# One kernel, its front's norm halves and weight sums issued in other rounds, and one more PSUM bank for the last chunk of rows

## The chip, the cores and the metric

The kernel runs on one core of one Trainium2 chip. The metric is the time of one execution on the device in microseconds (us); the time before is the median of three runs. A profile is one more execution, recorded by the hardware profiler; its times count from the start of its span.

The engines have short names in the profile: PE is TensorE (matmuls; PEld is its weight load, which overlaps them), DVE is VectorE, ACT is ScalarE, POOL is GpSimd, SP is SyncE, whose queue issues nearly all transfers here.

## The reference

A residual stack of four layers over `x` of shape 2 x 2048 x 256, in float32. Each layer norms its input and adds its result to `x`:

```python
x = x + scan_layer(layernorm(x), gamma, w_qkva)       # rmsnorm, q*scan(sigmoid(a), kv)
x = x + ffn(layernorm(x), W1, b1, W2, b2)             # 256 -> 1024 -> gelu -> 256
x = x + linear_attention(layernorm(x), W_q, W_k, W_v, W_o)   # 16 heads of 64, a running state
x = x + ffn(layernorm(x), W1, b1, W2, b2)
```

In `ffn` the weights are ternary: each is rounded to -1, 0 or 1 after division by the mean of the absolute values.

## The kernel before

The 4096 rows are 32 chunks of 128 rows. Four chunks make a block of 512 rows, and there are eight blocks, which alternate between the two batches (`blocks`, line 110). All of `x` stays on the chip in `x_sb`, each layer adding to it in place.

There are three parts. `front` (lines 557 to 738) does the scan layer and the first ffn. `attention` (lines 748 to 1196) does the third layer in 32 steps and begins the last ffn. A loop at the end (lines 1346 to 1367) does the rest of the last ffn. In all three PE, DVE, ACT and POOL execute their instructions in the order in which the code issues them (`by_hand`, line 1314), save for a few statistics that the program builder draws forward; only SP's transfers are ordered by a scheduler. So where a call stands in the code is where its instructions stand in each engine's queue, and an instruction that waits holds up all behind it on its engine.

The second half of `front` is a loop over eight rounds `i` (line 670). Round `i` does the ffn of block `i`:

- `ffn_in` (line 502): eight steps `f`, each with four matmuls of 128x512 into one bank (line 509), then the gelu on ACT (line 515). After each second step the 128x1024 result `h` is split: ACT casts it to `hh` (line 488), DVE subtracts to get the rest `hl` (line 494). Two buffers `h` take turns, so the gelu of steps 4 and 5 waits until the first `hl` is done.
- `ffn_out` (line 520): eight steps of eight matmuls (line 531), each of a step's four chunks with `hh` and with `hl`, into two banks of two chunks. DVE adds the banks to `x_sb` (line 540). In the last block of the last ffn the order is different: chunks 0 to 2 run through all eight `f` first, then chunk 3 alone, and each bank is added and stored as soon as it is complete. There chunk 2 and chunk 3 are the halves of one bank.
- `ffn_bias` (line 545): POOL adds `b2` to the rows of the next block, one 128x1024 instruction.

The input of `ffn_in` is made rounds ahead by four calls. `fs_` takes the statistics (four pairs of small DVE instructions, then four small ones on POOL, the last of which, `nb`, line 180, ACT waits for). `fr_`, in `fq_`, lets ACT write the normed rows `xn` (line 194). `fq_` goes on to turn them: DVE transposes 32x32 squares (line 259), SP writes them to DRAM in one transfer and reads them back in four. `fe_` splits what came back into halves: ACT casts to `xh` (line 202), DVE subtracts to `xl` (line 203). The halves of blocks 3 and 5 lie in the room of the weight `wq`, which is loaded from DRAM when round 5 has read them (line 704).

In rounds 0 to 3 the scan layer of later blocks is woven in; rounds 4 to 7 are the ffn alone.

Attention multiplies by a seven-product scheme (`Seven`, line 773). It needs sums of its weights: `weights_kv` (line 462) makes four POOL instructions of 128x512 for each of `wk`, `wv`, `wq`. They are issued in `ffn_out` of rounds 4, 5 and 6 (line 712, through the list at line 1330). It also needs sums `S` of the normed input (`pair_sums`, line 760: four POOL instructions of 128x128). The first of these stand at the start of attention; they wait for the last round's matmuls, since `S` takes over room that `hl` had. The first three products that PE does there are `hkN_Y` and `hkN_X`, which need no sum, and then `hkN_Z`, which needs the first of `S` and of `wk_t`.

Attention's own first rows (the chunk pair 0) are made in `front` by three calls: `then[0]` is `attention_stats` in round 6 after four steps of `ffn_in`, `then[1]` is `attention_rows` in `ffn_out` of round 6 (ACT writes two `xn`, DVE transposes them into `first_squares`, SP writes and reads back), and `then[2]` is `attention_turned` in round 7 (ACT copies to `xnT_first`). The statistics of the second pair of chunks are taken at the start of attention (line 994); their four small POOL instructions follow those of `S`.

Of the kernel before, what the change touches and what calls it, by code (L numbers as in the profile page):

```python
# [20 lines left out]
ALU = mybir.AluOpType  # L21
AX = mybir.AxisListType

P = 128
B, T, D = 2, 2048, 256
ND = D // P
FF = 4 * D
NF = FF // P
# [16 lines left out]
def kernel(  # L45
# [15 lines left out]
    nc = tc.nc  # L61
# [25 lines left out]
    wq = None  # L87
    wk = const.tile([P, ND, H * DK], FP, tag="wk", name="wk")
    w2 = const.tile([P, NF, D], FP, tag="wv", name="w2_in")
    wv = None  # L90
# [352 lines left out]
    def ffn_weights_away():  # L443

        for nm, w in (("w1r", w1r), ("w2r", w2r)):
            kept[nm] = dram.tile(w.shape, FP, tag=f"d{nm}", name=f"d{nm}")
            nc.sync.dma_start(out=kept[nm], in_=w.bitcast(FP))
# [14 lines left out]
    def weights_kv(w, t):  # L462
        l, r = slice(0, HK), slice(HK, H * DK)
        B11, B12, B21, B22 = w[:, 0, l], w[:, 0, r], w[:, 1, l], w[:, 1, r]
        T1, T2, T3, T4 = t[:, 0, :], t[:, 1, :], B12, t[:, 2, :]
        nc.gpsimd.tensor_tensor(T1, B12, B11, ALU.subtract)
        nc.gpsimd.tensor_tensor(T2, B22, T1, ALU.subtract)
        nc.gpsimd.tensor_tensor(T3, B22, B12, ALU.subtract)
        nc.gpsimd.tensor_tensor(T4, B21, T2, ALU.subtract)
# [50 lines left out]
    def ffn_out(g0, hid, store=False, tag="ps"):  # L520

        banks = [bank([P, 2, D], f"o{g0}_{i}", tag) for i in range(2)]
        if store and g0 == blocks[-1]:
            order = [(f, range(BC - 1)) for f in range(NF)] + [(f, range(BC - 1, BC)) for f in range(NF)]
        else:
            order = [(f, range(BC)) for f in range(NF)]
        for f, cs in order:
            for c in cs:
                to = banks[c // 2][:, c % 2, :]
                for k, h in enumerate((hid.hi, hid.lo)):  # L530
                    nc.tensor.matmul(  # L531
                        to, lhsT=h[f // 2][:, f % 2, c * P : (c + 1) * P], rhs=w2r[:, f, :],
                        start=(f == 0 and k == 0 and c % 2 == 0), stop=(f == NF - 1 and k == 1),
                        skip_group_check=True,
                    )
                m = 1 if len(cs) < BC and c > 1 else 2
                if f == NF - 1 and (c % 2 == 1 or m == 1):
                    g = g0 + c + 1 - m
                    xs = x_sb[:, g : g + m, :]
                    nc.vector.tensor_tensor(xs, xs, banks[c // 2][:, c % 2 + 1 - m : c % 2 + 1, :], ALU.add)  # L540
                    if store:
                        nc.sync.dma_start(out=rows(of, g, m), in_=xs)
            yield

    def ffn_bias(g0):

        xs = x_sb[:, g0 : g0 + BC, :]
        nc.gpsimd.tensor_tensor(xs, xs, b2_sb.unsqueeze(1).to_broadcast([P, BC, D]), ALU.add)

    def run(steps, n=None):  # L550
        for _ in steps if n is None else zip(range(n), steps):
            pass
# [4 lines left out]
    def front(scan_pool, ffn_pool, tern_pool, then, later):  # L557
# [21 lines left out]
        def fs_(i, between=None):  # L579
            fst[i] = norm_stats(ffn_pool, chunks(blocks[i]), bias=True, between=between)  # L580
# [4 lines left out]
        def fq_(i, to=ffn_pool, tag="raw"):  # L585
            fr_(i)
            src = fn[i].rearrange("t c (d b i) -> t b (c d) i", d=ND, b=NQ)
            nm = f"xn{blocks[i]}"
            fn[i] = squares_in(to, nm, squares_out(ffn_pool, nm, [src], 1), 1 if to is ffn_pool else None, tag)

        def fe_(i):
            if i > 5 and i % 2:
                room = [scan_pool.tile([P, ND, BT], FR, tag="kq", name=f"{t}{blocks[i]}") for t in ("xh", "xl")]
            elif i % 2:
                room = const.tile([P, 2, ND, BT], FR, tag="wq", name=f"xhl{blocks[i]}")
                room = [room[:, k] for k in range(2)]
            else:
                room = rows_room(ffn_pool, blocks[i], bufs=1)
            fn[i] = halves_end(fn[i], room)
# [70 lines left out]
        for i in range(NB):  # L670
            u, g0 = i + 5, blocks[i]
            more, scans = i + 1 < NB, u < len(units)
            hid, staged = hidden(ffn_pool, g0)
            steps = ffn_in(g0, fn.pop(i), hid, staged)
            if i == 0:
                ffn_bias(g0)
            if scans:
                ys[u] = []
                products = scan_steps(scan_pool, units[u][0], xnT[u], last[units[u][0] // CPB], ys[u])
                for j in range(4):  # L680
                    run(products, 1)
                    run(steps, 1)
                    if i == 0 and j == 0:
                        a_(4)
                        fq_(1)
                run(products)
                if i == 3:
                    fq_(5, scan_pool, "xn")
            else:
                run(steps, 4)  # L690
                if i == 4:
                    fs_(7)
                if i == NB - 2:
                    then[0]()
            if u + 1 < len(units):
                s_(u + 1)
            if i == 0:
                fs_(2)
            run(steps)
            if u + 1 < len(units):  # L700
                r_(u + 1)
            if i == 5:
                wq = const.tile([P, ND, H * DK], FP, tag="wq", name="wq")
                nc.sync.dma_start(out=wq, in_=w_q.rearrange("(c p) e -> p c e", p=P))
            if not more:
                wo = const.tile([P, NPR, D], FP, tag="wo", name="wo")
                nc.sync.dma_start(out=wo, in_=w_o.rearrange("(c p) e -> p c e", p=P))
                then[2]()

            steps = ffn_out(g0, hid, tag="out")  # L710
            if i > 3 and i - 4 < len(later):
                later[i - 4]()
            if i == 2:
                ffn_weights_away()
            if scans:
                fe_(i + 1)
                run(steps, 2)
                a_(u)
                run(steps, 3)
                if u + 1 < len(units):  # L720
                    t_(u + 1)
            if i < 3:
                fq_(i + 2)
                fs_(i + 3)
                if i == 2:
                    fs_(6)
            elif i == 3:
                fq_(6)
                fe_(5)
            elif i + 2 < NB:  # L730
                fe_(i + 2)
                if i + 3 < NB:
                    fq_(i + 3)
            if i == NB - 2:
                then[1]()
            run(steps)
            if more:
                ffn_bias(blocks[i + 1])

# [6 lines left out]
    def attention(keep, pool, state, last):  # L748
# [11 lines left out]
        def pair_sums(n):  # L760

            x = pairs[n]
            S = pool.tile([P, 4, P], FP, tag="S", bufs=1, name=f"S{n}")
            l, r = slice(0, P), slice(P, 2 * P)
            x11, x12, x21, x22 = x[:, 0, l], x[:, 1, l], x[:, 0, r], x[:, 1, r]
            for o, a, b_, op in (
                (S[:, 0, :], x21, x22, ALU.add), (S[:, 1, :], S[:, 0, :], x11, ALU.subtract),
                (S[:, 2, :], x11, x21, ALU.subtract), (S[:, 3, :], x12, S[:, 1, :], ALU.subtract),
            ):
                nc.gpsimd.tensor_tensor(o, a, b_, op)  # L770
            pairs[n] = x, S
# [219 lines left out]

        NS = len(steps)
        pair_sums(0)
        stats = norm_stats(norm_pool, pair(1), bias=True)
        k, q, v = Seven(0, "kN", "oT"), Seven(0, "qT", "uT"), Seven(0, "vN", "oT")
        k.go(2, 1, 0, 5)
# [203 lines left out]
    def pair(n):  # L1200
        return [b * CPB + n for b in range(B)]
# [115 lines left out]
    with (  # L1317
        tc.tile_pool(name="scan", bufs=2) as scan_pool,
        tc.tile_pool(name="ffn1", bufs=2) as ffn_pool,
        tc.tile_pool(name="tern", bufs=2) as tern_pool,  # L1320
        tc.manual_schedule(engines=by_hand),
    ):

        warm = bank([P, P], "warm")
        for _ in range(12):
            nc.tensor.matmul(warm, lhsT=ones, rhs=ones, start=True, stop=True)
        nc.scalar.activation(table, ones[:, :1], AF.Sigmoid)
        front(
            scan_pool, ffn_pool, tern_pool, (attention_stats, attention_rows, attention_turned),
            [lambda: weights_kv(wk, wk_t), lambda: weights_kv(wv, wv_t), lambda: weights_kv(wq, wq_t)],  # L1330
        )
    front_ctx.close()

# [71 lines left out]
```

## Time and profile before

| what | us |
|---|---|
| runs | 1059.29, 1057.63, 1059.35 |
| median of the runs | 1059.29 |
| the profiled execution, its own time | 1060.83 |
| its span | 1059.0 |
| round 3, matmuls of `ffn_out` begin | 157.71 |
| rounds 4, 5, 6, 7 begin | 166.06, 182.89, 198.71, 213.64 |
| attention begins | 228.60 |
| last matmul of attention before the last loop, about | 945 |
| last block's `ffn_out` begins | 1046.72 |
| last matmul begins | 1055.54 |

The profile's windows give, for a stretch of time, its length and each engine's busy time in it (in brackets the number of instructions), then the granted TensorE clock, the DMA share and the rate. The timeline gives an instruction's start, its length (of a run of the same ones together, with their number), and in square brackets how long its engine had been idle before it and which instruction ended that. The chain is the work that ended last, each piece followed back to what released it.

### The profile page before, as it was taken

How to read it: one execution, taken by the hardware profiler on the slowest of the kernel's cores; microseconds unless marked ns; L12 is line 12 of the kernel's file. 1: busy time of each engine (PE TensorE's matmuls, PEld its weight loads, DVE VectorE, ACT ScalarE, POOL GpSimd, SP SyncE). 2: the span in 40 equal slices, each digit the busy share in tenths (PEclk: the TensorE clock that was granted, in tenths of full speed). 3: DMA queues.
4: the chain of work that ended last, by engine and by line, in shares of the span. 5: the costliest groups of instructions: out<-in, count | busy, mean ns of one | idle time of the engine just before them, and what ended most of it. 6: DMA issues, size and time to landing. Idle time of an engine off the chain costs nothing.

```text
span 1059.0 us, 43544 instructions
## 1 busy us (share of the span) xinstructions
PE 1044.0 (99%) x19920; PEld 805.4 (76%) x19920; DVE 730.8 (69%) x1047; ACT 613.4 (58%) x813; POOL 201.7 (19%) x314
## 2 busy tenths in 40 slices
PE   9999999999999999999999999999999999999998
PEld 7567778886777777777777777777777777889887
DVE  7987788856676765767666667666576666668873
ACT  4567778755645555455554555545545454658974
POOL 3433242831101001011010110100101020035540
PEclk9999999999999999999999999999999999999999
DMA  9231112203442423423324243243341334223321
GB/s 312 81 119 41 40 41 81 80 20 122 141 135 71 138 95 115 140 77 129 131 75 142 93 132 113 82 133 103 122 136 69 123 122 132 73 82 120 119 81 41
DMA packets 80825, 111.23 MB, mean 105 GB/s; under 512 B 8320, under 2 KB 66560, under 8 KB 80384
## 3 DMA queue, kind: packets, MB, share of 16 engines
q1 hardware_dynamic: 79024, 106.07, 30.2%
q8 instruction: 156, 2.56, 1.0%
q10 hardware_dynamic: 1584, 2.36, 0.9%
q14 instruction: 29, 0.24, 0.1%
q0 software_dynamic: 32, 0.00, 0.0%
HBM read 57.81 MB, written 50.59 MB: 102 GB/s over the span
## 4 chain that ended last, share of the span: by engine, by line
PE 90%; DVE 3%; ACT 2%; issue 2%; DMA 2%; POOL 1%; SPq 0%; ACTq 0%; DVEq 0%
PE hy L952 11%; PE o L531 9%; PE h L509 8%; PE hkN_X L818 6%; PE hqT_X L813 6%; PE hp L872 6%; PE hvN_X L818 6%; PE pq L368 4%; PE pq L388 3%; PE hS L929 3%; PE huT L889 3%; PE hoT L889 3%; PE huT L903 3%; PE hM L929 3%; PE hoT L903 3%; PE hqT_Z L813 3%
## 5 line engine op out<-in xcount | busy, mean ns | idle before, releaser
L878 DVE TENSOR_TENSOR p<-hp,mask 128x512 f32<-128x512 f32 x128 | 82.3, 683 | 83.4 <-PE hp L872 83.4
L952 PE MATMUL hy<-wo,oT 128*128 128x256 f32 x512 | 124.2, 386 | 0.0
L770 POOL TENSOR_TENSOR S<-xnT 128x128 f32<-128x128 f32 x30 | 13.8, 460 | 516.1 <-ACT xnT L312 516.1
L952 PEld LDWEIGHTS hy<-wo,oT 128*128 128x128 f32 x512 | 93.5, 190 | 20.6 <-issue 8.5
L494 DVE TENSOR_TENSOR hl<-h,hh 128x1024 fp32r<-128x1024 f32 x60 | 84.6, 1420 | 29.5 <-ACT hh L488 29.3
L515 ACT ACTIVATE h<-h,b_sb 128x512 f32<-128x512 f32 x120 | 77.9, 683 | 38.6 <-PE h L509 36.1
L914 ACT COPY uT<-huT 128x512 f32<-128x512 f32 x32 | 18.7, 586 | 124.9 <-PE huT L903 124.9
L194 ACT ACTIVATE xn<-x_sb,nb,rs 128x256 f32<-128x256 f32 x124 | 65.7, 594 | 21.9 <-POOL nb L180 20.1
L941 DVE TENSOR_TENSOR S<-S,hS 128x512 f32<-128x512 f32 x60 | 41.2, 687 | 43.2 <-PE hS L929 40.2
L259 DVE STREAM_TRANSPOSE squN<-uT 128x1024 f32<-128x1024 f32 x31 | 63.6, 2053 | 5.4 <-ACT uT L916 4.9
L971 ACT COPY uN<-rawuN 128x1024 f32<-128x1024 f32 x31 | 64.5, 2082 | 4.5 <-DMA rawuN<-dsquN 4.1
L259 DVE STREAM_TRANSPOSE sqkT<-kN 128x1024 f32<-128x1024 f32 x32 | 65.9, 2059 | 1.3 <-ACT kN L849 1.2
L971 ACT COPY kT<-rawkT 128x1024 f32<-128x1024 f32 x32 | 66.7, 2084 | 0.0
L488 ACT CAST hh<-h 128x1024 fp32r<-128x1024 f32 x60 | 63.1, 1051 | 1.9
L531 PE MATMUL o<-w2r,hl 128*128 128x256 f32 x256 | 61.3, 282 | 1.5 <-DVE hl L494 1.3
L531 PE MATMUL o<-w2r,hh 128*128 128x256 f32 x256 | 61.3, 281 | 0.0
L531 PE MATMUL o<-w2r_back,hh 128*128 128x256 f32 x248 | 60.4, 284 | 0.9 <-DVE x_sb L540 0.9
L531 PE MATMUL o<-w2r_back,hl 128*128 128x256 f32 x248 | 60.0, 281 | 0.0
L849 ACT COPY vN<-hvN_X 128x512 f32<-128x512 f32 x16 | 9.4, 587 | 78.8 <-PE hvN_X L818 78.8
L162 DVE BATCH_NORM_STATS2 st<-x_sb 128x6 f32<-128x256 f32 x128 | 51.2, 401 | 2.4 <-DMA x_sb<-in_x_dram 2.3
L823 DVE TENSOR_TENSOR kN<-kN,hkN_Y 128x512 f32<-128x512 f32 x16 | 11.0, 687 | 57.2 <-ACT kN L832 57.2
L531 PEld LDWEIGHTS o<-w2r,hl 128*128 128x128 f32 x256 | 48.2, 188 | 2.9 <-DVE hl L494 2.4
(227 smaller groups left out, 2554.3 us busy)
## 6 DMA issues: line engine op xcount, KB each, us to landing
dsqkT<-sqkT SPq DMA_DIRECT2D x32, 512.0 KB, 3.3
rawkT<-dsqkT SPq DMA_DIRECT2D x128, 128.0 KB, 3.0
dsquN<-squN SPq DMA_DIRECT2D x31, 512.0 KB, 3.3
rawuN<-dsquN SPq DMA_DIRECT2D x124, 128.0 KB, 3.1
dsqxn<-sqxn SPq DMA_DIRECT2D x14, 512.0 KB, 2.7
rawxn<-dsqxn SPq DMA_DIRECT2D x56, 128.0 KB, 2.9
out_dram<-x_sb SPq DMA_DIRECT2D x15, 256.0 KB, 2.9
x_sb<-in_x_dram SPq DMA_DIRECT2D x7, 512.0 KB, 8.9
```

Of the source, the lines that this page charges most:

```text
L194: nc.scalar.activation(xn[:, c, :], x_sb[:, g, :], AF.Identity, bias=nb[:, c : c + 1], scale=rs[:, c : c + 1],)
L259: nc.vector.transpose(to, src)
L494: nc.vector.tensor_tensor(self.lo[a], h, self.hi[a], ALU.subtract)
L509: nc.tensor.matmul(ph, lhsT=w1r[:, d, f * P : (f + 1) * P], rhs=r[:, d, :], start=(d == 0 and k == 0), stop=(d == ND - 1 and k == 1),)
L515: nc.scalar.activation(h[:, f % 2, :], ph, AF.Gelu, bias=b1_sb[:, f : f + 1])
L531: nc.tensor.matmul(to, lhsT=h[f // 2][:, f % 2, c * P : (c + 1) * P], rhs=w2r[:, f, :], start=(f == 0 and k == 0 and c % 2 == 0), stop=(f ...
L813: nc.tensor.matmul(to[:, j, :], lhsT=self.B[i][:, j * P : (j + 1) * P], rhs=self.A[i], start=(new and j == 0), stop=True, skip_group_check ...
L818: nc.tensor.matmul(to, lhsT=self.A[i], rhs=self.B[i], start=new, stop=True, skip_group_check=True)
L872: nc.tensor.matmul(banks[h][halves[c], p, :], lhsT=d[s][left][halves[h], p, halves[c]], rhs=d[s]["qT"][halves[h], p, halves[c]], start=Tru ...
L878: nc.vector.tensor_tensor(d[s][nm][:, h], banks[h], mask8, ALU.mult)
L952: nc.tensor.matmul(py, lhsT=d[s]["oT"][:, p, :], rhs=wo[:, p, :], start=(p == 0), stop=(p == NPR - 1),)
L971: act(t, d[s]["r" + nm].rearrange("p t q -> p q t"))
```

## The change

It has five parts, in the order of the rounds.

1. `fe_(5)` goes from `ffn_out` of round 3 to `ffn_out` of round 4, where `fe_(6)` follows it as before.
2. For block 7, `fs_` goes from the middle of `ffn_in` in round 4 to the start of `ffn_in` in round 5, `fq_` from `ffn_out` of round 4 to that of round 5, and `fe_` from `ffn_out` of round 5 to that of round 6. On SP the load of `wq` now stands before block 7's transfers.
3. `attention_stats` goes from `ffn_in` of round 6 to its `ffn_out`, behind `fe_(7)`; `attention_rows` goes from `ffn_out` of round 6 to `ffn_in` of round 7, behind its second step.
4. The sums of `wk` and `wq`, eight POOL instructions, go to the end of round 6, behind `ffn_bias(7)`. Those of `wv` go into attention, between the first `S` and the statistics of the second pair.
5. In the last block of the last ffn, chunk 3 gets a bank of its own.

On POOL the order from round 3 to attention is then: the bias of block 4, that of block 5, the statistics of block 7, the bias of block 6, attention's statistics, the bias of block 7, four sums of `wk`, four of `wq`, four of `S`, four of `wv`, the second pair's statistics.

```diff
@@ ffn_out
         if store and g0 == blocks[-1]:
             order = [(f, range(BC - 1)) for f in range(NF)] + [(f, range(BC - 1, BC)) for f in range(NF)]
+            banks.append(bank([P, 2, D], f"o{g0}_2"))
         else:
             order = [(f, range(BC)) for f in range(NF)]
         for f, cs in order:
             for c in cs:
-                to = banks[c // 2][:, c % 2, :]
+                at = c // 2 if len(cs) > 1 else 2
+                to = banks[at][:, c % 2, :]
                 for k, h in enumerate((hid.hi, hid.lo)):
                     nc.tensor.matmul(
                         to, lhsT=h[f // 2][:, f % 2, c * P : (c + 1) * P], rhs=w2r[:, f, :],
-                        start=(f == 0 and k == 0 and c % 2 == 0), stop=(f == NF - 1 and k == 1),
+                        start=(f == 0 and k == 0 and (c % 2 == 0 or at == 2)), stop=(f == NF - 1 and k == 1),
                         skip_group_check=True,
                     )
...
-                    nc.vector.tensor_tensor(xs, xs, banks[c // 2][:, c % 2 + 1 - m : c % 2 + 1, :], ALU.add)
+                    nc.vector.tensor_tensor(xs, xs, banks[at][:, c % 2 + 1 - m : c % 2 + 1, :], ALU.add)
@@ front, ffn_in of rounds 4 to 7
             else:
+                if i == 5:
+                    fs_(7)
+                elif not more:
+                    run(steps, 2)
+                    then[1]()
                 run(steps, 4)
-                if i == 4:
-                    fs_(7)
-                if i == NB - 2:
-                    then[0]()
@@ front, ffn_out
             steps = ffn_out(g0, hid, tag="out")
-            if i > 3 and i - 4 < len(later):
-                later[i - 4]()
             if i == 2:
                 ffn_weights_away()
+            if i == 4:
+                fe_(5)
...
             elif i == 3:
                 fq_(6)
-                fe_(5)
-            elif i + 2 < NB:
-                fe_(i + 2)
-                if i + 3 < NB:
-                    fq_(i + 3)
-            if i == NB - 2:
-                then[1]()
+            elif i == 4:
+                fe_(6)
+            elif i == 5:
+                fq_(7)
+            elif i == 6:
+                fe_(7)
+                then[0]()
             run(steps)
             if more:
                 ffn_bias(blocks[i + 1])
+            if i == 6:
+                later()
@@ attention
         pair_sums(0)
+        weights_kv(wv, wv_t)
         stats = norm_stats(norm_pool, pair(1), bias=True)
@@ the call of front
-            [lambda: weights_kv(wk, wk_t), lambda: weights_kv(wv, wv_t), lambda: weights_kv(wq, wq_t)],
+            lambda: (weights_kv(wk, wk_t), weights_kv(wq, wq_t)),
```

## The prediction

> **What bounds the kernel now.** I read the page's totals and its chain first.
>
> ```profile
> PE 1044.0 (99%) x19920; PEld 805.4 (76%) x19920; DVE 730.8 (69%) x1047; ACT 613.4 (58%) x813; POOL 201.7 (19%) x314
> PE 90%; DVE 3%; ACT 2%; issue 2%; DMA 2%; POOL 1%; SPq 0%; ACTq 0%; DVEq 0%
> ```
>
> PE sets the end; time is won only where PE waits. So I took the windows of rounds 4 to 7 (start and end of each, its length, PE's busy time).
>
> ```profile
> 166.06:182.89 16.83, 15.50 (x99) 13.58 (x97) 13.95 (x18) 14.77 (x17) 4.44 (x6) 1.00 0.23 71
> 182.89:198.71 15.82, 15.64 (x99) 13.69 (x97) 15.33 (x9) 12.17 (x15) 15.74 (x8) 1.00 0.38 133
> 198.71:213.64 14.93, 14.93 (x99) 13.48 (x98) 10.80 (x17) 10.17 (x14) 10.33 (x9) 1.00 0.01 1
> 213.64:228.60 14.96, 14.96 (x98) 13.49 (x97) 6.93 (x7) 10.10 (x13) 4.76 (x3) 1.00 0.11 36
> ```
>
> A round without a wait is 14.93 us long (7.46 in, 7.47 out). Round 4 is 1.90 longer, round 5 0.89. The timelines of PE, DVE and POOL there say why.
>
> ```profile
> 170.06 2.29 DVE L203 TENSOR_TENSOR xhl<-rawxn,xhl 128x1024 fp32r<-128x1024 f32 x1 [1.41 <-ACT xhl L202]
> 173.45 2.37 DVE L494 TENSOR_TENSOR hl<-h,hh 128x1024 fp32r<-128x1024 f32 x2
> 174.74 0.38 PE L531 MATMUL o<-w2r,hl 128*128 128x256 f32 x1 [0.94 <-DVE hl L494]
> 179.12 0.38 PE L531 MATMUL o<-w2r,hl 128*128 128x256 f32 x1 [0.39 <-DVE hl L494]
> ...
> 187.50 7.06 DVE L494 TENSOR_TENSOR hl<-h,hh 128x1024 fp32r<-128x1024 f32 x3
> 191.20 2.27 POOL L466 TENSOR_TENSOR wv_t<-wv 128x512 f32<-128x512 f32 x1
> 193.55 2.15 POOL L467 TENSOR_TENSOR wv_t<-wv,wv_t 128x512 f32<-128x512 f32 x1
> 195.66 2.26 POOL L468 TENSOR_TENSOR wv<-wv 128x512 f32<-128x512 f32 x1
> 212.25 1.29 POOL L467 TENSOR_TENSOR wq_t<-wq,wq_t 128x512 f32<-128x512 f32 x1
> 216.00 2.40 POOL L548 TENSOR_TENSOR x_sb<-x_sb,b_sb 128x1024 f32<-128x1024 f32 x1
> 217.51 1.97 DVE L494 TENSOR_TENSOR hl<-h,hh 128x1024 fp32r<-128x1024 f32 x1 [2.79 <-ACT hh L488]
> 228.90 0.46 POOL L770 TENSOR_TENSOR S<-xnT_first 128x128 f32<-128x128 f32 x1 [10.50 <-PE o L531]
> ```
>
> In round 4, `fe_(5)`'s subtraction waits on ACT and a transfer, so the first `hl` comes late. In round 5 subtractions and POOL's sums stretch each other: three `hl` take 7.06, against 1.23 for one alone, and a sum of `wv` 2.15 to 2.27, against 1.29 for one of `wq`. The starts interlock: an `hl` ends, a sum runs about 1.1, the next `hl` about 1.1. At 217.51 `hl` sat until the bias ended at 218.40 (1.97 less 0.89 is 1.08). I model the two as taking turns, whole instructions each. DVE's transposes and its adds out of PSUM show no stretch beside POOL.
>
> The tail, PE's timeline:
>
> ```profile
> 1052.42 0.28 PE L531 MATMUL o<-w2r_back,hl 128*128 128x256 f32 x1
> 1053.64 0.39 PE L531 MATMUL o<-w2r_back,hh 128*128 128x256 f32 x1 [0.94 <-DVE x_sb L540]
> ```
>
> Chunk 3 waits until DVE has read chunk 2 from the shared bank.
>
> **The change, part by part.** Times are us; R4 to R8 are the starts of rounds 4 to 7 and of attention.
>
> *The bank.* From 1052.42 to 1053.64 is 1.22; matmuls there start every 0.12. The bank removes 1.10, and all behind it (add, store, 3.4 to the span's end) moves up: **-1.1**. The new bank comes from the ring of `h`, last read by a gelu of that round, long before.
>
> *Round 4.* `fe_(5)` leaves the place ahead of the round's gelus on ACT and `hl` on DVE, and block 7's statistics leave DVE (175.72 to 177.88, the 0.39 wait). Both waits go: **-1.90**. What is late next is `fe_(5)` itself, now needed at once. By round 7's rows the last cast `hh` ends at R+10.5; a cast by ACT 2.3, a subtraction 2.2: ready at R4+15.1, against PE's first use of the low half at 14.93+0.23. I take +0.1 (0 to 0.6, if a queue slips half a microsecond). `fe_(7)` at the end of round 6 is the same case: +0.1. POOL's bias of block 5 now follows that of block 4 at once, at 159.0, ahead of an `hl` at 159.17: that one ends near 162.5, PE needs it at 162.3: **+0.2** (0 to 0.3). Issuing `wq` ahead of block 7's transfers on SP is free: it waits for R5+7.5, block 7's for DVE at R5+15.5; turned in 8.4 (159.35 to 167.73) they are back by R6+9, needed at R6+10.5.
>
> *Round 5* gets `fe_(6)`'s subtraction, the two adds (1.2) and block 7's statistics (2.1) ahead of its first `hl`, which then ends at R5+6.8, needed at 7.6. POOL's four small ones take 2.9 beside an `hl` (178.12 to 180.98): the bias of block 6 runs 8.6 to 10.95. The third `hl`, ready at 9.1, sits behind it and ends at 12.05; PE needs it at 11.3. With the restart that is a wait of 0.85 where there was 0.89: **0** (-0.9 if the bias misses that `hl`, +0.2).
>
> *Round 7 and the entry of attention.* The eight sums of `wk` and `wq` now stand between `attention_stats` and `S` on POOL. `fe_(7)` ends at R7+0.1, the statistics on DVE 1.65 later, POOL's four 1.6 (230.80 to 232.42): 3.4. The bias of block 7 takes 2.35: 5.75. Then by turns: first `hl` (ready 3.9) to 6.9, a sum to 8.0, `hl` to 9.1, sum to 10.2, `hl` to 11.3, sum to 12.4, `hl` to 13.5, sum to 14.6; four sums of `wq` alone, 5.12 (210.88 to 216.00): 19.7. `S` then starts at R7+19.8, not at R8+0.3. `attention_rows` costs ACT 1.09 behind the first cast and DVE a transpose of 1.10, inside slacks of 1.2 to 2.0 that `hl` had in round 7; its transfers need 5.5 (213.2 to 218.7) and are back at 13.6. The last `hl` is some 0.4 late for PE, so R8 is R7+15.3. Whatever R8 is, PE does `hkN_Y` and `hkN_X` (0.86 each) and then needs the first `S`, done at 20.3, plus 0.5 from weight load to matmul: 20.8. Without any wait `hkN_Z` would start at 14.93+1.72, 16.65. Together **+4.1**. Behind `hkN_Z` all products stand in PE's order, so nothing makes it up. From below: eight sums at 1.28 and no turns end at 16.0, the first `S` is done at 16.5, and with the 0.5 the cost is 0.3. From above: eight at the mean of the four of `wv` (2.46, the last was 3.15) end at 25.4, cost 9.8. I take the turns, since the rows interlock and only four `hl` are there.
>
> *`wv` in attention.* Four sums (5.1) behind `S`: the first is needed 13.4 behind R8 (`hvN_Z`, 241.95), more than 10 after it is done. The second pair's POOL four come 5.1 later, ready about 8.2 behind `S`'s start; ACT wants them 9.1 after it (238.00 against 228.90): 0, but with `S` on time a slack of under 1.
>
> The granted clock is 1.00 in all windows above. The Trainium skill, "TensorE: Matmul & The Clock Gate", section "Why this matters for your kernels", says to leave PE no idle gap over about 3 us, or it falls back to half its clock. No row shows such a fall. By that rule the wait at attention's entry could cost up to 1.7 more, an estimate from the page's 3.4 us window.
>
> **Sum:** -1.1 - 1.9 + 0.1 + 0.1 + 0.2 + 0 + 4.1 = +1.5 on the span of 1059.0. The profiled execution was timed at 1060.83, 1.8 around its span and above all three runs; I carry the difference to the median, 1059.29: **1060.8**.
>
> **The rivals.** *Faster: the sums fit.* If subtractions and sums do not take turns in round 7, the entry costs 0.3: 1.5 - 4.1 + 0.3 = -2.3, 1057.0; with round 5's wait gone as well 1056.1. For it: sums of `wq` at 1.29. Against it: no row has a sum beside an `hl` at 1.29.
>
> *Slower: POOL's queue at the entry.* The same place, dearer: at 2.46 a sum the entry costs 9.8 and the whole comes to +7.2, 1066.5. It decides from where `S` starts 0.6 later than I say, beyond R7+20.4 (+2.1 in all). For it: `wv`'s fourth sum at 3.15, and a chain of some fifteen POOL instructions, each slip of which PE pays in full. Against it: `wq`'s four have no `hl` beside them.
>
> *It doesn't relieve round 4.* Four engines follow the written order, so the waits can only return as lateness of `fe_(5)`: at its bound of 0.6 on both such places, +1.0 more and 1061.8: slower, if only just.
>
> **How the numbers follow.** The forecast has 0.54, the faster rival 0.19, the slower one 0.22 and a late `fe_` 0.05. A run of this kernel tells about 0.2% (2.1 us) from no change, so the forecast of +1.5 is within it, and the chance of slower is the last two together, 0.27. The range goes from 1056.0, just under the faster rival with round 5 free as well, to 1064.0, about half way from the forecast to the slower rival; the forecast's own is 1058.8 to 1061.4.
>
> **What would show it.** Right: round 4 at 15.0, round 5 near 15.8, no gap at the tail, `S` starting about R7+20 with eight sums before it, the first four near 2.2 apart, and an `hkN_Z` that waits over 3 us for POOL. Wrong: `S` within 1 us of R8, or sums at 1.29 beside `hl`; or new waits at R5 and R7 of over 0.6, for `xhl` or `xl`.

## The result, and the profile after

| what | before | after |
|---|---|---|
| median of the runs, us | 1058.95 (8 runs, 1057.47 to 1059.71) | 1062.38 (8 runs, 1060.61 to 1064.39) |
| ratio | | 1.0039, 95% interval 1.0027 to 1.0051 |
| the profiled execution, its own time | 1060.83 | 1060.61 |
| its span | 1059.0 | 1058.8 |
| rounds 4, 5, 6, 7 begin | 166.06, 182.89, 198.71, 213.64 | 165.91, 180.85, 196.47, 211.40 |
| attention begins | 228.60 | 226.81 |
| first `S` begins, behind the start of round 7 | 15.26 | 19.52 |
| `hkN_Z` begins, behind attention's start | 1.72 | 4.61 |
| last block's `ffn_out` begins | 1046.72 | 1047.73 |

The change is slower by 0.3 to 0.5%. The two spans alone would say that nothing happened: the profiled execution of before lay 1.9 above its median, that of after 1.8 below its own. So the traces are read step by step here, and why the executions scatter is taken up with the experiments.

The page of after, its totals and the engines' shares of the chain:

```profile
PE 1045.7 (99%) x19920; PEld 806.6 (76%) x19920; DVE 729.5 (69%) x1047; ACT 612.6 (58%) x813; POOL 198.2 (19%) x314
PE 92%; POOL 2%; ACT 2%; DVE 2%; issue 1%; POOLq 0%; ACTq 0%
```

PE sets the end as before, and POOL's share of the chain went from 1% to 2%. The windows of rounds 4 to 7 (start and end, length, busy time of PE, PEld, DVE, ACT and POOL, granted clock):

```profile
165.91:180.85 14.94, 14.94 (x99) 13.48 (x97) 10.99 (x11) 13.34 (x14) 0.00 (x0) 1.00 0.28 90
180.85:196.47 15.62, 15.24 (x99) 13.62 (x97) 13.13 (x17) 11.17 (x16) 6.73 (x5) 1.00 0.19 67
196.47:211.40 14.93, 14.93 (x98) 13.47 (x97) 8.49 (x9) 11.17 (x13) 0.00 (x0) 1.00 0.22 72
211.40:226.81 15.41, 15.35 (x98) 13.54 (x96) 11.73 (x16) 11.18 (x15) 13.51 (x10) 1.00 0.11 35
```

Round 4 is down to the 14.94 of a round without a wait, round 5 has one wait left, and in round 7 POOL is busy nearly throughout, where it had 4.76. The timeline of after, POOL, DVE and PE in round 5, then POOL from round 7 on and PE at attention's start:

```profile
190.08 3.36 POOL L550 TENSOR_TENSOR x_sb<-x_sb,b_sb 128x1024 f32<-128x1024 f32 x1
192.20 2.33 DVE L494 TENSOR_TENSOR hl<-h,hh 128x1024 fp32r<-128x1024 f32 x1 [1.02 <-ACT hh L488]
194.58 0.39 PE L533 MATMUL o<-w2r,hl 128*128 128x256 f32 x1 [0.38 <-DVE hl L494]
...
214.57 2.40 POOL L550 TENSOR_TENSOR x_sb<-x_sb,b_sb 128x1024 f32<-128x1024 f32 x1
216.92 2.29 POOL L466 TENSOR_TENSOR wk_t<-wk 128x512 f32<-128x512 f32 x1
...
223.66 2.26 POOL L469 TENSOR_TENSOR wk_t<-wk,wk_t 128x512 f32<-128x512 f32 x1
225.89 1.29 POOL L466 TENSOR_TENSOR wq_t<-wq 128x512 f32<-128x512 f32 x1
...
229.70 1.26 POOL L469 TENSOR_TENSOR wq_t<-wq,wq_t 128x512 f32<-128x512 f32 x1
230.92 0.45 POOL L775 TENSOR_TENSOR S<-xnT_first 128x128 f32<-128x128 f32 x1
231.42 2.07 PE L823 MATMUL hkN_Z<-wk_t,S 128*128 128x512 f32 x2 [2.63 <-POOL S L775]
233.29 1.66 PE L818 MATMUL hqT_Y<-xnT_first,wq 128*128 128x128 f32 x8
...
236.54 1.02 PE L823 MATMUL hkN_Z<-wk,S 128*128 128x512 f32 x2
```

The same three products in the timeline of before:

```profile
230.32 1.02 PE L818 MATMUL hkN_Z<-wk_t,S 128*128 128x512 f32 x2
231.18 1.05 PE L813 MATMUL hqT_Y<-xnT_first,wq 128*128 128x128 f32 x8
...
233.82 1.02 PE L818 MATMUL hkN_Z<-wk,S 128*128 128x512 f32 x2
```

The sums of `wk` take 2.16 to 2.29 each while DVE has `hl` to do, those of `wq` 1.26 to 1.29 when it has none left; `S` stands behind all eight, and PE idles 2.63 for it. But `hkN_Z` then takes 2.07 where it took 1.02, and `hqT_Y` 1.66 where it took 1.05. The windows around that place tell why (the column behind the busy times is the granted clock):

```profile
227.70:231.10 3.40, 1.10 (x3) 0.19 (x1) 0.77 (x2) 0.58 (x1) 3.40 (x4) 1.00 0.00 0
231.15:234.55 3.40, 3.13 (x8) 2.09 (x9) 0.00 (x0) 0.58 (x1) 3.24 (x6) 0.50 0.00 0
234.60:238.00 3.40, 3.40 (x17) 2.21 (x17) 0.33 (x1) 1.17 (x2) 3.32 (x4) 1.00 0.00 0
```

Behind the idle time PE had half its clock for 3.4 us. Of these it worked 3.13, so some 1.6 are lost on top of the wait.

The tail, from the chain of after (start, length, what):

```profile
1047.89 7.73 PE o L533 x64
1055.65 0.42 DVE x_sb L542
```

The 64 matmuls of the last `ffn_out` run through without the wait in their middle.

Against before, step by step: -0.15 ahead of round 4, round 4 -1.89, round 5 -0.20, round 7 +0.45, the late `S` +2.89, half clock +1.62. That is +2.72, and so much later does the second `hkN_Z` start (236.54 against 233.82). From 333 to 549 us the products are 3.11 late; the other 0.4 comes at about 293 and 307 us, where PE makes short stops of the kind that is taken up at the end of the experiments. With the tail's -1.10 that makes **+2.0**, against +3.4 between the medians.

### The profile page after: what moved, and what is told of

Read it like the earlier page. It is cut to its first block, busy times and chain, and to the rows that moved or that the text cites. A ratio compares the mean times of both kernels' runs of the same rounds, so it can differ in the third digit from the quotient of the medians.

```text
span 1058.8 us, 43547 instructions
## 1 busy us (share of the span) xinstructions
PE 1045.7 (99%) x19920; PEld 806.6 (76%) x19920; DVE 729.5 (69%) x1047; ACT 612.6 (58%) x813; POOL 198.2 (19%) x314
## 4 chain that ended last, share of the span: by engine, by line
PE 92%; POOL 2%; ACT 2%; DVE 2%; issue 1%; POOLq 0%; ACTq 0%
PE hy L957 11%; PE h L509 9%; PE o L533 9%; PE hp L877 6%; PE hkN_X L823 6%; PE hqT_X L818 6%; PE hvN_X L823 6%; PE pq L368 4%; PE pq L388 4%; PE hoT L894 3%; PE hS L934 3%; PE huT L894 3%; PE huT L908 3%; PE hoT L908 3%; PE hM L934 3%; PE hkN_Z L823 3%
## 5 line engine op out<-in xcount | busy, mean ns | idle before, releaser
L957 PEld LDWEIGHTS hy<-wo,oT 128*128 128x128 f32 x512 | 93.5, 190 | 19.5 <-issue 7.4
L175 POOL TENSOR_TENSOR rs<-rs,mhalf 128x2 f32<-128x2 f32 (+1 forms) x49 | 43.7, 891 | 35.6 <-DVE rs L172 32.3
```

The costliest lines, as they stand in the source:

```text
L957: nc.tensor.matmul(py, lhsT=d[s]["oT"][:, p, :], rhs=wo[:, p, :], start=(p == 0), stop=(p == NPR - 1),)
```

## The experiments

Each of e1 to e7 and of e10 to e12 was run 7 to 12 times, beside 24 to 35 runs of the kernel before on the same chip (its medians there: 1058.57 for e1 to e4, 1059.73 for e5 to e7, 1058.71 for e10 to e12). e8 and e9 are one run each. "By the steps" is what the products from 333 to 549 us and the tail show in the trace.

**e1: the eight sums one round earlier.** Against the changed kernel:

```diff
-            if i == 6:
+            if i == 5:
                 later()
```

> The changed kernel with one edit: the eight sums of wk and wq are issued at the end of round 5 (behind the bias of block 6), not at the end of round 6. Theory A (the first S is late because POOL is still at the sums, and the idle PE then loses its clock): S starts within 0.5 us of attention's first matmul, hkN_Z follows hkN_X without a wait, the granted clock is 1.000, and all that the entry cost in the changed kernel's profile goes (0.45 in round 7, 2.89 before hkN_Z, 1.62 at the low clock): 5.0 us less than the changed kernel's 1062.4, so about 1057.4; round 6 may give 0 to 0.6 back, since sums and subtractions then take turns there. Theory B (the slowdown comes from waits in attention for which the profile names nothing, which differ from run to run): the entry is repaired in the trace all the same, but the time stays at 1061 to 1063.

Measured: 1057.4, ratio to before 0.9986 (0.997 to 1.0001). The timeline of e1:

```profile
226.67 0.46 POOL L775 TENSOR_TENSOR S<-xnT_first 128x128 f32<-128x128 f32 x1 [9.68 <-PE o L533]
...
228.19 1.02 PE L823 MATMUL hkN_Z<-wk_t,S 128*128 128x512 f32 x2
```

POOL is idle 9.68 before `S`, `hkN_Z` neither waits nor runs at half clock, and the products are 1.8 ahead of before instead of 3.1 behind. By the steps e1 is 2.9 faster than before and the change 2.0 slower; the 4.9 between them are round 7, the late `S` and the half clock (0.45, 2.89 and 1.62). So the loss of the change is at this one place, and the time came out at the 1057.4 that had been expected.

**e2: the wait is left, PE's idle time is filled.** Against the changed kernel; a product is done over into the same bank, so the result is the same:

```diff
-        k.go(2, 1, 0, 5)
+        k.go(2)
+        for _ in range(3):
+            nc.tensor.matmul(k.Y, lhsT=k.A[2], rhs=k.B[2], start=True, stop=True, skip_group_check=True)
+        k.go(1, 0, 5)
```

> The changed kernel with three more copies of the product hkN_Y (3 x 0.86 us of matmuls into the same bank, same result) ahead of hkN_X, so that PE works through most of the time in which it waits for S. Theory A1 (the idle gap of 3.6 us lowers the clock): S starts as late as before, but the gap is under 1.2 us, the granted clock is 1.000 and the products after it take 0.86 and 0.89 again; 1.6 us less, about 1060.8. Theory A2 (the clock falls for another reason, or the slow products are waits): no change, 1062.4, clock 0.998. If S were not what PE waits for, the copies would add 2.6: 1065.

Measured: 1060.23, ratio 1.0008 (0.9998 to 1.0019). The timeline of e2:

```profile
227.66 2.74 PE L1004 MATMUL hkN_Y<-wk,xnT_first 128*128 128x512 f32 x6
...
231.04 0.45 POOL L775 TENSOR_TENSOR S<-xnT_first 128x128 f32<-128x128 f32 x1
231.54 1.13 PE L823 MATMUL hkN_Z<-wk_t,S 128*128 128x512 f32 x2 [0.28 <-POOL S L775]
```

And its windows there and at a wait much later:

```profile
230.00:234.00 4.00, 3.72 (x15) 1.94 (x14) 0.69 (x1) 1.17 (x2) 3.92 (x6) 1.00 0.00 0
...
904.00:908.00 4.00, 1.63 (x93) 1.49 (x92) 1.01 (x2) 2.60 (x2) 0.00 (x0) 0.97 0.48 156
908.00:912.00 4.00, 4.00 (x52) 3.39 (x49) 1.29 (x2) 0.68 (x1) 0.00 (x0) 0.60 0.51 133
```

`S` and `hkN_Z` come as late as in the changed kernel, but the clock stays at 1.00 and `hkN_Z` takes 1.13: products at 234 us are 1.32 behind before, not 2.72. So the half clock comes from PE's idle time and costs 1.4 here. The runs agree: a mean clock of 0.998 or less stands in 24 of the 32 runs of kernels that have the whole wait (the changed one, e5 and e11 below) and in 2 of the 12 of e2. At 905 PE is idle 2.37 without a named cause, and there the clock falls too.

**e3: the tail's bank alone**, part 5 of the change on the kernel before.

> The kernel before with the last chunk's own bank alone. Theory: the gap of 1.22 us between chunk 2's last matmul and chunk 3's first becomes 0.12, and the time falls by 1.1, from 1058.95 to 1057.85 (to be seen in the trace exactly, in the times only within the scatter). Rival: the store or the add behind it is the bound, and less than 0.5 is left of it.

Measured: 1057.21, ratio 0.9993 (0.9979 to 1.0006). The gap of the tail is gone from the trace, and the two waits of round 4 are there (1.24 and 0.39; 0.94 and 0.39 in before). A gain of 1.1 is within what the runs allow, and so is none.

**e4: the sums alone**, part 4 of the change on the kernel before.

> The kernel before with the move of the weight sums alone (wk and wq at the end of round 6, wv in attention). Theory A: round 5 loses the sums' turns with its subtractions (0 to 0.9 gained), the entry of attention costs as in the changed kernel (S some 2 us late, a wait of 2.5 to 3.5 at hkN_Z, the low clock 1.6): 4 to 5 us slower than before, 1063 to 1064. Theory B (the entry is not what makes the changed kernel slower): within 1 us of before, 1059.

Measured: 1059.04, ratio 1.0009 (0.9996 to 1.0021). Theory A missed by 4 to 5; theory B's time came, though not for its reason, since e1 shows that the entry is where the changed kernel loses. The timeline of e4:

```profile
209.20 2.40 POOL L548 TENSOR_TENSOR x_sb<-x_sb,b_sb 128x1024 f32<-128x1024 f32 x1
211.57 1.29 POOL L466 TENSOR_TENSOR wk_t<-wk 128x512 f32<-128x512 f32 x1
...
223.40 2.27 POOL L469 TENSOR_TENSOR wq_t<-wq,wq_t 128x512 f32<-128x512 f32 x1
...
227.23 0.46 POOL L769 TENSOR_TENSOR S<-xnT_first 128x128 f32<-128x128 f32 x1 [1.56 <-PE o L531]
```

Here `attention_stats` is still in `ffn_in` of round 6, so POOL is through with it early: the bias of block 7 starts 5.4 sooner than after the whole change, and the sums end before attention begins (226.94). This points at part 3, the statistics behind `fe_(7)`, which e6 tests.

**e5: the changed kernel once more**, on the chip of e6 and e7.

> The changed kernel itself once more, beside the kernel before on one chip. By the steps of the two traces the changed kernel should be 2.0 us slower (its products in attention start 3.1 later from 330 us to 550 us, the tail gives 1.1 back). Theory A (the rest of the 3.4 that was measured is scatter of waits that differ from run to run): 1.5 to 2.5 us slower than before on this chip. Theory B (the change costs something more that the profiled execution did not show): 3 to 4 slower again. The granted clock is under 1.000 in every run.

Measured: 1064.05 (1060.43 to 1065.69), ratio 1.0022 (1.0003 to 1.0041). The late `S` is there again (230.98). The medians are 4.3 apart, which looks like theory B, but the interval of the ratio, 0.3 to 4.3 us, holds both theories. "In every run" was wrong for the clock: 8 of 12 runs show a mean granted clock of 0.997 or 0.998, which is one or two stretches of 3.4 at half clock (3.4 x 0.5 is 1.7, 0.16% of the span), and 4 runs show 1.000 (4 of 12 in e11 too). So this idle time did not lower the clock every time, or was not there every time; which of the two, no trace shows.

**e6: `attention_stats` back in `ffn_in` of round 6.** Against the changed kernel:

```diff
                 run(steps, 4)
+                if i == 6:
+                    then[0]()
...
                 fe_(7)
-                then[0]()
```

> The changed kernel with attention_stats back in ffn_in of round 6, where the kernel before has it; the sums stay at the end of round 6. Theory A (POOL is late because attention_stats, behind fe_(7), opens its queue only 1.7 us into round 7; e4 had the early statistics and no late S): S starts within 0.5 us of attention's first matmul and the clock stays at 1.000, which is worth 5.0; but the bias of block 7 and the sums now take turns with the last hl of round 6 (0.9 late for PE) and with fe_(7)'s subtraction, which round 7 needs at once (1.2 late): 2.9 us less than the changed kernel in all. Theory B (the eight sums are too many wherever they begin): S still over 2 us late.

Measured: 1058.99, ratio 0.998 (0.996 to 1.0), 5.1 below the changed kernel on the same chip (3.5 by the steps; 2.9 had been expected). The first `S` starts at 228.30, 0.3 behind attention's start, and `hkN_Z` does not wait; instead PE waits at the start of round 7 (timeline of e6):

```profile
213.10 0.50 PE L509 MATMUL h<-xl,w1r 128*128 128x512 f32 x1 [1.16 <-DVE xl L203]
...
228.30 0.46 POOL L776 TENSOR_TENSOR S<-xnT_first 128x128 f32<-128x128 f32 x1 [1.29 <-PE o L533]
```

DVE begins `xl` at 209.34 (209.18 in the changed kernel), but now beside the bias of block 7 (POOL, 208.79 to 211.18), and the subtraction takes 3.71 in place of 2.19. That is the other side of part 3: it keeps `fe_(7)` just in time, and pays with POOL's queue.

**e7: the sums in round 5, ahead of the bias.** Against the changed kernel:

```diff
             run(steps)
+            if i == 5:
+                later()
             if more:
                 ffn_bias(blocks[i + 1])
-            if i == 6:
-                later()
```

> As e1 (the eight sums at the end of round 5), but ahead of the bias of block 6. Theory: the third hl of round 5 waits for at most one sum (1.1) where it waited for the bias (2.4), so round 5 goes from 15.46 to 15.0 at most; in round 6 each hl waits for at most one sum or the bias and PE waits for none; S is there with attention's first matmul. 0.4 less than e1, so 3.3 us less than before by the trace, to be seen in the times within their scatter: about 1056. Rival: the turns only move to round 6, and nothing is won over e1.

Measured: 1058.49, ratio 0.9969 (0.9951 to 0.9987), faster than both kernels. Round 5 has no wait any more, but attention's start has a new one (timeline of e7):

```profile
226.31 1.12 PE L823 MATMUL hkN_Y<-wk,xnT_first 128*128 128x512 f32 x2 [0.39 <-ACT xnT_first L312]
```

Round 5 takes 14.94 in place of e1's 15.62, round 7 15.52 in place of 14.96, so most of the gain is given back, and the products are 1.79 ahead of before, as in e1 (1.81). By the steps nothing is won over e1, which is what the rival said, though it put the loss in round 6.

**What makes the executions scatter.** In every trace PE waits in attention at places for which the profile names no cause ("issue"). They come to 6.5 in the profile of before and 3.6 in that of after. In the timeline of before and of after:

```profile
290.13 1.11 PE L929 MATMUL hM<-vN,uN 64*64 64x64 f32 x64
292.67 1.12 PE L818 MATMUL hkN_X<-wk_t,S 128*128 128x512 f32 x2 [1.43 <-issue]
```

```profile
292.90 1.11 PE L934 MATMUL hM<-vN,uN 64*64 64x64 f32 x63
295.30 0.27 PE L934 MATMUL hM<-vN,uN 64*64 64x64 f32 x1 [1.29 <-issue]
```

After 63 of 64 like matmuls there is no operand left to wait for. The page of after has one more line, among the DMA queues (packets, MB, share of the engines' span):

```profile
q8 instruction: 156, 2.56, 1.0%
```

These are transfers of 16384 bytes each, and PE does 19920 matmuls: 128 of them for each transfer (19920 / 156 is 127.7). Set beside the packets of that queue in the trace, the unnamed waits of after are:

```
PE stops   PE restarts   an instruction transfer has landed   restart behind it
294.01     295.30        293.88                               1.42
632.25     632.66        631.27                               1.39
828.72     829.41        827.82                               1.59
873.94     874.43        873.16                               1.27
906.22     906.89        905.50                               1.39
```

In the 14 traces of this case there are 70 unnamed waits of 0.35 or more in attention (240 to 945 us), and 68 of them end 1.2 to 1.6 behind such a landing (the other two 1.0), though the landings are 5 us apart in the mean (141 from 240 to 945 us). So PE seems to run out of instructions. Five kernels test it by moving PE's stream of instructions against the program.

**e8 and e9: 24 and 48 small matmuls more at attention's start**, on the kernel of e1 (e8 has 11, e9 has 23 narrow ones and each a wide one; each counts twice):

```diff
-        k.go(2, 1, 0, 5)
+        k.go(2)
+        for n in [64] * 11 + [HK]:
+            nc.tensor.matmul(k.Y[:, :n], lhsT=k.A[2], rhs=k.B[2][:, :n], start=True, stop=True, skip_group_check=True)
+        k.go(1, 0, 5)
```

> The kernel with the sums at the end of round 5, and 24 small matmuls more on PE at the start of attention (a product done over; the result is the same). It is run for where PE's unnamed waits lie, not for its time. Theory P (the unnamed waits are PE's instructions arriving late: the page lists 156 transfers of 16384 bytes on the instruction queue for 19920 matmuls, which is one for each 128 matmuls, and in the profiles so far nearly every unnamed wait ended 1.25 to 1.6 us behind the end of such a transfer): the waits stay at their place in PE's stream and so move 24 matmuls ahead in the program. The one near 290, between matmul 63 and 64 of hM in that kernel, then lies between 39 and 40 of hM, 0.8 to 1.8 long; every unnamed wait over 0.4 between 240 and 945 ends 1.2 to 1.6 behind the end of an instruction transfer; the wait of huT for ACT (0.67 near 279) stays at the first huT. Rival Q (the wait belongs to that product or its data, or is made of matmul records that are missing): hM is split 63 and 1 as before, wherever PE's stream stands. Time by both: 1 to 4 above the kernel without the 24 matmuls, within the scatter of one run.

> The same with 48 small matmuls more instead of 24. Theory P: the wait near 290 lies between matmul 15 and 16 of hM, the other unnamed waits 48 matmuls further ahead in the program than without the addition, each ending 1.2 to 1.6 behind the end of an instruction transfer. Rival Q: hM is split 63 and 1, or not at all.

Measured: 1058.55 both. `hM` runs through without a wait in either. Theory P missed the place in both; rival Q missed it in e8, and in e9 "not at all" was one of the two outcomes that it named. The unnamed waits that are left come to 1.3 and 1.1, and all but one end 1.3 to 1.5 behind a landing. The added matmuls took 3.5 and 6.2, yet the kernels took only 0.3 more than the 1058.23 of before on that chip (one run each).

**e10, e11, e12: the stream moved by 24 at no cost**, on the kernel before, on the changed one and on e1. PE does 24 matmuls while it waits for its first data; here it does 48 narrow ones:

```diff
-        for _ in range(12):
-            nc.tensor.matmul(warm, lhsT=ones, rhs=ones, start=True, stop=True)
+        for _ in range(24):
+            nc.tensor.matmul(warm[:32, :64], lhsT=ones[:, :32], rhs=ones[:, :64], start=True, stop=True)
```

> The kernel before with 48 small matmuls (32x64) in place of the 24 of 128x128 that PE does while it waits for its first data, and nothing else: PE's stream from there on stands 24 matmuls further on. Theory P (PE waits where a whole piece of 128 instructions of its stream falls on a dense run of 64x64 matmuls, since the next piece is not there yet): as in the two runs with 24 and 48 matmuls added at attention's start, the unnamed waits in attention come to 1 to 3 in all in place of 5 to 6.5, the one near 290 is gone, and the median is 2 to 4 below the kernel before. Rival Q (such waits lie where they lie by chance, and the two runs were lucky): unnamed waits of 4 to 6.5, the time within 1 of before. If the small matmuls take longer than the 0.7 that PE has to spare at the start, up to 1.5 more by both.

> The changed kernel with the same 48 small matmuls at the start. It shows what the change is worth when PE's stream is cut elsewhere. By the steps of the two traces (round 4 -1.90, round 5 -0.36, round 7 +0.45, late S +2.89, half clock +1.62, tail -1.10, other 0.4) it is 2.0 above the kernel before with the same addition; if the change itself lost 3.4 (as the medians said, without the unnamed waits' part in it), it is 3.4 above. By theory P it is below the changed kernel's own difference to before: 0 or less against before; by Q 2 to 4 above before.

> The kernel with the sums at the end of round 5 (no late S) and the same 48 small matmuls at the start. By the steps 2.9 below the kernel before with the same addition. By theory P some 5 below before, about 0.995, and faster than any kernel so far; by Q 1 to 3 below before, as it was without the addition.

| | median, us | ratio to before |
|---|---|---|
| e10, before with 48 | 1057.13 (1056.07 to 1059.05) | 0.9983 (0.9973 to 0.9994) |
| e11, after with 48 | 1060.14 (1057.93 to 1062.78) | 1.0014 (1.0004 to 1.0024) |
| e12, sums in round 5, with 48 | 1056.34 (1053.37 to 1057.37) | 0.997 (0.9958 to 0.9982) |

It had been expected that the wait near 290 would be gone. It is still there, but it has moved in the program. The timelines of e10, of e11 and of e2, which has 6 matmuls more than the changed kernel:

```profile
288.87 0.76 PE L929 MATMUL hM<-vN,uN 64*64 64x64 f32 x40
290.69 0.58 PE L929 MATMUL hM<-vN,uN 64*64 64x64 f32 x24 [1.06 <-issue]
```

```profile
294.31 0.76 PE L934 MATMUL hM<-vN,uN 64*64 64x64 f32 x39
296.64 0.62 PE L934 MATMUL hM<-vN,uN 64*64 64x64 f32 x25 [1.57 <-issue]
```

```profile
291.60 1.03 PE L934 MATMUL hM<-vN,uN 64*64 64x64 f32 x57
293.75 0.34 PE L934 MATMUL hM<-vN,uN 64*64 64x64 f32 x7 [1.12 <-issue]
```

24 matmuls more ahead of it: 64 became 40, and 63 became 39. Six more: 63 became 57. The wait stays where it is in PE's stream and not at a product.

The other waits say the same. Of all the instructions that PE's queue has in a trace (39959 in that of after: weight loads, matmuls and 119 others, nearly all for semaphores), 156 transfers are one for 256. Counted from the start, each of the 70 unnamed waits of the 14 traces comes at place 192 or 193 of its 256, whatever the product; the 31 waits with a named cause (0.34 or more, from 200 to 1050 us) come at places from 14 to 229. In e8 and e9 PE reached that place in `hM` 2.0 and 2.3 us after the landing, later than the 1.2 to 1.6 at which the waits end, and did not wait.

In e10, e11 and e12 the unnamed waits come to 3.3 to 3.6: at the low end of the kernels without the addition (3.4 to 7.1), and above the 1 to 3 expected. The kernel before gained 1.6 in the median, 0.6 to 2.9 by the ratio's interval, less than the 2 to 4 expected; e12 is 2.4 below before in place of some 5, and e11 above before in place of level with it. By the steps e12 was to lie 2.9 below e10, and the medians differ by 0.8. So the places follow the theory, and the sizes fall short of it by about half or more. Nor is all of e10's gain made by the unnamed waits: in its profile round 4 takes 15.51 in place of 16.83, because a transfer landed earlier.

Between e11 and e10, the same change on the moved stream, lie 3.0. The profile of e11 shows the half clock twice as long (its windows):

```profile
230.50:234.00 3.50, 2.72 (x6) 1.69 (x7) 0.00 (x0) 0.58 (x1) 3.34 (x7) 0.50 0.00 0
234.00:237.50 3.50, 3.50 (x13) 2.47 (x13) 0.00 (x0) 0.58 (x1) 3.50 (x3) 0.52 0.00 0
```

## Why the prediction was right, and where it was short

The forecast was 1060.8; the runs gave 1062.38, inside the range, though above the 1058.8 to 1061.4 of the forecast itself. The mechanism came as told, with one term missing. That the named steps of the trace come to +1.6 (+2.72 and the tail's -1.10) where the sum said +1.5 is luck: the missing half clock, +1.62, stands against +0.4 that was set aside and not needed, 0.35 more gained up to round 5, and 0.76 less lost at attention. Two of the signs named for "right" came smaller: round 5 took 15.62 for "near 15.8", and `hkN_Z` waited 2.63, not over 3.

- *The tail, round 4 and the just-in-time halves.* -1.10 and -1.89 came as worked out; the 0.4 set aside for `fe_(5)`, `fe_(7)` and the bias of block 5 were not needed, since none of these waits came. But the round 4 of before that was read is one draw. In the four traces with `fe_(5)` in round 3 (before, e3, e4, e10) it took 16.83, 17.09, 16.35 and 15.51: ACT's cast there waits for a transfer and began at 167.73, 167.73, 166.95 and 166.43. In the ten others it took 14.92 to 14.94. So this part is worth 0.6 to 2.2, and 1.5 in the mean of the four.
- *Round 5.* Forecast 0, found -0.20. A wait of PE for an `hl` behind the bias is there, but for the fourth `hl` and not the third: the bias began at R5+9.2 beside the third, took 3.36 and held the fourth until R5+12.6. PE is idle 0.38 for it, and the round is 0.69 longer than one without a wait, in place of the 0.85 foreseen.
- *Turns on DVE and POOL.* Right in kind and size: four sums at 2.16 to 2.29, four at 1.26 to 1.29, `S` at R7+19.5 against R7+19.8. The rival with sums that fit is out. The slower rival's place was right, but it was to decide beyond R7+20.4, which was not reached.
- *The wait at attention.* Round 7 gave +0.45 and `S` +2.89, 3.34 against the +4.1 forecast; 0.5 had been added for a weight load which in the trace took 0.04 (`S` done 231.38, `hkN_Z` 231.42).
- *The missing term.* The half clock, +1.62. The sum left it out, because no row of before had an idle time of that length. The Trainium skill, "TensorE: Matmul & The Clock Gate", section "Why this matters for your kernels", gave the rule, and the estimate from it was up to 1.7; the traces agree in the size (half clock for 3.4 us), and e2 shows that the idle time is the cause. Its limit of about 3 us is too high here: idle times of 2.63, 2.85 and 2.37, by the profile's account, were enough, and in e5 one of 1.75 was followed by half clock too; in attention none of 1.57 or less was.
- *What the late `S` needs.* The prediction put it down to the sums' place. e4 and e6 show that the sums without the late statistics don't do it, and e1 that the late statistics without the sums there don't: it takes both.
- *From a span to the medians.* I carried a sum of steps to the median of before. The steps of the trace are +2.0, or +2.4 with the mean of the four rounds 4 in place of the one that was read. The medians differ by 3.4 (2.9 to 5.4 by the ratio's interval), in e5 by 4.3 (0.3 to 4.3 by the interval of the ratio), in e11 against e10 by 3.0. A part of the rest are runs in which the half clock lasts twice as long, as in the profile of e11, or comes again behind an unnamed wait, as in that of e5 (another 3.4 from 296.7); but such runs are 3 of 32. What the rest is stays open.

## What to carry to other kernels

An instruction that is moved is paid for by whoever stands behind it in that engine's queue: before eight sums go ahead of a short one that the next stage waits for, count when the queue opens, not only how long they take. An idle time of 2.4 to 2.9 us on PE cost more than itself in most runs here (24 of 32), since the matmuls behind it ran at half clock for 3.4 us; filling it with work that is thrown away won 1.4 us back here. And a profile's span is one draw: compare the steps, and take medians of runs for the whole.

## What the runs showed that was not expected

- PE's waits without a named cause end 1.2 to 1.6 behind the landing of a 16384-byte instruction transfer (68 of 70), and all 70 stand at one place in 256 instructions of PE's stream. The one at `hM` keeps that place when matmuls are added ahead of it (e2, e10, e11, e12). Most lie in or just behind a run of 64x64 matmuls, 64 in 1.1 us. In these traces they take 1.1 to 7.1 in an execution, up to about twice what the change costs. So PE waits there for its own instructions: nothing else in the record comes once in 256 of them. No run took the transfers away.
- An instruction transfer took 0.98 in the median of the 14 traces where no other transfer ran beside it, 1.13 where others kept the 16 engines busy for over 60% of its time, and 2.8 at most.
- Moving PE's stream by 24 matmuls, in time that PE had to spare, made the kernel before faster by 0.06 to 0.27%, with no other edit; what of this the unnamed waits made is not shown. With the sums in round 5 as well (e12) the ratio is 0.997 (0.9958 to 0.9982), no different from e7's 0.9969 without it; which of the two is faster was not measured side by side.
